# Attention logits of a two-layer graph network: FP32 products of 64 rows replaced by FP32R products of two-part queries and stacked two-part keys, with a smaller ring for software DMA

## The chip, the cores and the metric

The kernel runs on one core of one Trainium2 chip. The metric is the device time of one execution in microseconds; lower is better. A core has five engines with queues of their own: PE (TensorE, matrix products; PEld are its weight loads), DVE (VectorE), ACT (ScalarE), POOL (GpSimd) and SP (SyncE, which here only issues DMAs). Each works through its instructions in the order in which they were written, and waits where an operand is not there yet.

## The reference

Two layers over 4096 nodes with 256 features. Layer 0 is a graph attention with 4 heads over a dense adjacency `adj`, a residual and a layer norm. Layer 1 does two steps of a bilinear attention that keeps, in each row, the largest probabilities up to a mass of 0.9, and beside it a plain mixing with the adjacency. What matters here is the attention of layer 1:

```python
def _top_p_attention(X, W1, W2, W3):
    q = X @ W1.T @ W2.T            # (4096, 64)
    k = X @ W3.T                   # (4096, 64)
    logits = q @ k.T / TAU         # (4096, 4096), contraction over 64
    probs = jax.nn.softmax(logits, axis=-1)
    ...                            # keep the largest up to TOP_P = 0.9
    return A / jnp.maximum(A.sum(-1, keepdims=True), 1e-12)
...
for n in range(STEPS):             # STEPS = 2
    A = _top_p_attention(Xa, W1, W2, W3)
    Xf = R @ Xf                    # R: rows of S + identity, normalised
    Xa = A @ Xa
    Z = Z + Xf @ U1[n].T + Xa @ U2[n].T
```

Then come a residual and two layer norms.

## The kernel before

`graph_attention` does layer 0. For each of 8 heads (two halves of the columns, four heads) it goes over 32 pieces of 128 rows; a piece is a masked choice on DVE (L604, L607, 2.6 us each), two activations on ACT (L582, L589) and products into `acc` (L634). The inputs of the projections come in eight blocks `xt`; four of these lie for a time in the tile `kT` (`load_xT`, L217 to L224), which is not needed for keys yet. When a block of 512 nodes is done, it is normalised, and `Keys` (L427 to L466) transposes it, multiplies it with `w3` and puts the keys into `kT`. `w3` holds the same 64 columns twice, so the product `kp` has the keys in rows 0 to 63 and again in rows 64 to 127 of PSUM. ACT copies one of the halves (`evict`, L463): `kT` has 128 rows and 2048 columns, with the keys of nodes 0 to 2047 in the upper 64 rows and those of nodes 2048 to 4095 in the lower 64.

`nucleus_layer` does layer 1 in two steps of 32 row tiles (`RowTile`). Its helper `keys` (L859 to L881) makes the keys of the second step in the same layout, with a DVE copy at the end. A row tile runs through this:

- the query: transpose, product with `w1` (`front_q1`), product with `w2`, twice the same 64 columns (`front_q`, L908 to L914), so that the 128 rows of `q` are the 64 numbers of a query twice. ACT copies it from the PSUM bank `misc`, which in step 2 also serves the final products `zp` (L1352).
- the logits, in four "pairs" (`logits`, L917 to L932): one FP32 product for the block `pair` with the upper 64 rows and one for the block `pair + 4` with the lower 64 rows. The two use different rows of the array. Each has its PSUM bank; there are two banks of this kind (`ps_lg`, tag `lg`). `logits_evict` (L934) is two copies on ACT from these banks to the row tile `p`.
- the largest values of each chunk of 128 (`tops`, L939), the maximum (`top`), the exponentials (`spread`, `exp`), an estimate of the threshold in a few rounds (`estimate`, on DVE; in step 2 `estimate_half`, two passes over 2048 columns on ACT, L1040 and L1043), the exact threshold (`final`, `sort`, `edge`), the choice (`select` in step 1; `inside` and `cut` in step 2).
- the product with the features: transposes `tpa` (L1216), copies `at`, and 32 FP32 products `ap` (L1234).

Beside it `Mix` multiplies the adjacency with the features, `rp` (L1294): for most tiles as an F32R product with a low part of 258 columns (`low`) and an F16 product with a high part of 256 columns; `place_out` adds the last products `zp` (L1355), and layer norms.

The order of all this on PE, ACT, DVE and POOL is written out by hand: `at(time, part)` puts a part on a plan, in units of one row tile; `carry_out` sorts the plan by time and emits it. The due times are in the tables `T1` (step 1) and `T2` (step 2) at L1405 to L1411. The times say only the order within each engine. DMAs are on SP, apart from 32 mask loads (L556) and 8 casts from memory to memory (L211) on POOL, which convert as they move and so go through software DMA; all 40 are in layer 0.

At the end a flag counts rows for which the choice could not be confirmed; if it is not zero, a branch (L162) computes everything again in a general way (`graph_attention` without the factors, `nucleus_general`).

Of the kernel before, what the change touches and what calls it, by code (L numbers as in the profile page):

```python
# [22 lines left out]
P = 128  # L23
# [3 lines left out]
DA = 64  # L27
# [57 lines left out]
@with_exitstack  # L85
def tile_graph_layers(
    ctx: ExitStack,
    tc: tile.TileContext,
    x: bass.AP,
    xT: bass.AP,  # L90
    adjT: bass.AP,
    W: bass.AP,
    a: bass.AP,
    bias: bass.AP,
    res_w: bass.AP,
    res_b: bass.AP,
    W1T: bass.AP,
    W2T: bass.AP,
    W3T: bass.AP,
    U1T: bass.AP,  # L100
    U2T: bass.AP,
    ln_g: bass.AP,
    ln_b: bass.AP,
    out: bass.AP,
):
# [44 lines left out]
    graph_attention(  # L150
        tc, x, xT, adjT, W, a, bias, res_w, res_b, ident, eps, w3, kT, xf, x1_d, src_d, mask_d, adj_d,
        narrow, load_weights,
    )
    flag = const.tile([P, 1], I32, name="flag")
    nucleus_layer(
        tc, adjT, adj_d, adj32_d, high_d, low_d, w1, w2, w3, kT, U1T, U2T, ln_g, ln_b, ident, eps,
        xf, room, x1_d, xf1_d, xa2_d, narrow, flag, out,
    )


    missed = nc.values_load(flag[0:1, 0:1], min_val=0, max_val=STEPS * N)
    with tc.If(missed != 0):  # L162
        xf = room("xf_again")[:, :, : D + 1]
        graph_attention(
            tc, x, xT, adjT, W, a, bias, res_w, res_b, ident, eps, w3, kT, xf, x1_d, src_d, mask_d, adj_d,
            None, None,
        )
        nucleus_general(
            tc, adjT, w1, w2, w3, kT, U1T, U2T, ln_g, ln_b, ident, eps, xf, x1_d, xf1_d, out
        )  # L170


# [5 lines left out]

@with_exitstack
def graph_attention(  # L180
    ctx, tc, x, xT, adjT, W, a, bias, res_w, res_b, ident, eps, w3, kT, xf, x1_d, src_d, mask_d, adj_d,
    narrow, load_more,
):


# [31 lines left out]
    def load_xT(b):  # L217
        if b % 4 > 1:

            t = kT[:, b % 2 * 1024 : (b % 2 + 1) * 1024].rearrange("p (c n) -> p c n", c=2)  # L220
# [181 lines left out]
    def normalise(t0):  # L402
# [21 lines left out]

        return rest

    class Keys:  # L427


# [238 lines left out]
    for head in heads:  # L668
# [26 lines left out]
        for b in range(HB):  # L695
            at(time + 4.9 + b, head.add, b)
            if head.h == H - 1:

                k = b if head.half else 4 * b
                at(time + 5.2 + k, head.normalise, b)  # L700
                at(time + 6.7 + k, head.normalise_rest, b)
                parts = Keys(head.half * HB + b)
# [32 lines left out]
def nucleus_layer(  # L735
# [123 lines left out]
    def keys(b):  # L859

        xt = []
        for c in range(2):
            tp = ps_tr.tile([P, 512], F32, tag="tr", name=f"tpk{b}_{c}")
            for q in range(4):
                nc.tensor.transpose(
                    tp[:, q * P : (q + 1) * P], xa[:, b * 4 + q, c * P : (c + 1) * P], ident
                )
            t = two.tile([P, 512], F32, tag="at", name=f"xkt{b}_{c}", bufs=3)
            if c:
                nc.scalar.copy(t, tp)  # L870
# [8 lines left out]
        half, at = divmod(b, NB // 2)  # L879
        rows = slice(half * DA, (half + 1) * DA)  # L880
        nc.vector.tensor_copy(kT[rows, at * 512 : (at + 1) * 512], kp[rows, :])  # L881

    class RowTile:

# [23 lines left out]
        def front_q(self):  # L908
            qp = ps_one.tile([P, 512], F32, tag="misc", name=f"qq{self.id}")
            nc.tensor.matmul(  # L910
                qp[:, :P], w2.rearrange("p k a -> p (k a)"), self.q1, start=True, stop=True
            )
            self.q = two.tile([P, P], F32, tag="q", name=f"q_{self.id}")
            nc.scalar.copy(self.q, qp[:, :P])  # L914


        def logits(self, pair):  # L917

            if pair == 0:
# [6 lines left out]
            at = slice(pair * 512, (pair + 1) * 512)  # L926
            self.lps[pair] = []
            for half in range(2):
                lp = ps_lg.tile([P, 512], F32, tag="lg", name=f"lp{self.id}_{pair}_{half}")
                rows = slice(half * DA, (half + 1) * DA)  # L930
                nc.tensor.matmul(lp, self.q[rows, :], kT[rows, at], start=True, stop=True)  # L931
                self.lps[pair].append(lp)  # L932

        def logits_evict(self, pair):  # L934
            for half, lp in enumerate(self.lps.pop(pair)):
                b = half * (NB // 2) + pair
                nc.scalar.copy(self.p[:, b * 512 : (b + 1) * 512], lp)  # L937

        def tops(self, src, b):  # L939
# [265 lines left out]


        def tops_of_pair(self, pair):
            for half in range(2):
                self.tops(self.p, half * (NB // 2) + pair)

        def product_transpose(self, b):
            if b == 0:
# [188 lines left out]
    def at(time, part, *args):  # L1401
# [7 lines left out]
        lag=0.218, out=0.344, qt=0.253, q1=0.460, q2=0.612, space=0.125, apart=0.250, split=0.300,  # L1409
    )  # L1410
    T2 = dict(top=0.481, spread0=0.650, spread1=0.518, exp0=0.653, exp1=0.593, scalars=0.728, scalars2=0.769, est0=0.800, join0=0.820, move0=0.835, join1=0.945, move1=1.068, est2=1.200, join2=1.232, move2=1.395, lift=1.497, final=1.643, tops=1.647, sort=1.827, edge=2.032, inside=2.121, cut=2.230, product=2.354, lag=0.090, out=0.060, qt=-0.077, q1=0.461, q2=0.489, space=0.067, apart=0.074, mix=0.576, copy=0.042)  # L1411

    def carry_out():
        for _, _, part, args in sorted(plan, key=lambda e: e[:2]):
# [553 lines left out]
```

## Time and profile before

| | |
|---|---|
| median of 3 runs | 3505.24 us (3499.11 to 3508.46) |
| the profiled execution | 3507.4 us |
| its span, first to last instruction | 3505.5 us |
| mean granted clock of PE | 0.954 |
| busy time of PE, PEld, DVE, ACT, POOL | 3219.6, 2073.3, 2862.1, 2526.9, 610.9 us |
| products `rp` L1294, low and high part | 558.5 and 497.3 us |
| products `ap` L1234, step 1 and step 2 | 495.5 and 490.8 us |
| logits `lp` L931, 1024 records | 343.7 us |
| copies of the logits L937, 512 | 273.7 us |

A line of a group reads: line, engine, operation, output<-inputs, partitions x elements and type, count | busy time and mean ns of one | idle time of the engine just before them and what ended it. An FP32 product leaves two records on PE, an F32R or F16 product one. The ends of products are modelled from their starts, so that the mean of one is more than the distance from one to the next; where it matters, starts are compared. The slices cut the span into 40 parts of 87.6 us; a digit is the busy share in tenths.

### The profile page before, as it was taken

What the parts mean: (1) busy time and instruction counts of PE and PEld (TensorE: products, weight loads), DVE (VectorE), ACT (ScalarE), POOL (GpSimd) and SP (SyncE); (2) the same over time, 40 slices, a digit from 0 to 9 for tenths busy, and PEclk for the clock granted to TensorE, in tenths of its full rate; (3) what the DMA queues carried; (4) which work ended last, traced back from release to release, by engine and by line L of the source; (5) the groups of instructions that cost most, each with busy time, mean ns of one, the idle gap of its engine ahead of it and who ended that gap; (6) DMA issues with size and microseconds to landing.
All of it is one profiled execution on the core that took longest, in us unless ns stands there. A gap on an engine that the chain in (4) does not pass through costs nothing. (4 is left out here: it accounts for less than half of the span.)

```text
span 3505.5 us, 55976 instructions
## 1 busy us (share of the span) xinstructions
PE 3219.6 (92%) x19538; PEld 2073.3 (59%) x19538; DVE 2862.1 (82%) x8615; ACT 2526.9 (72%) x3970; POOL 610.9 (17%) x435
## 2 busy tenths in 40 slices
PE   8998888888789999999997899999899999999997
PEld 4522222222357777777774666666677777767775
DVE  4779989999658888888624998989989999988993
ACT  4678889888668888888715777777777677667752
POOL 1101450000000000000000222222223332332332
PEclk9999999999889999999998999999899999999988
DMA  9846443332242222222236444444644444444443
GB/s 213 136 113 140 128 133 119 110 112 85 74 132 103 106 82 103 106 94 92 100 99 165 120 113 118 121 117 120 166 104 109 109 118 107 112 108 108 111 106 82
DMA packets 637300, 402.58 MB, mean 115 GB/s; under 512 B 262672, under 2 KB 588304, under 8 KB 633936
## 3 DMA queue, kind: packets, MB, share of 16 engines
q1 hardware_dynamic: 626640, 315.03, 31.8%
q10 hardware_dynamic: 1536, 67.11, 5.3%
q0 software_dynamic: 8832, 16.78, 5.2%
q8 instruction: 155, 2.54, 0.3%
q14 instruction: 137, 1.12, 0.1%
HBM read 406.03 MB, written 118.62 MB: 150 GB/s over the span
## 5 line engine op out<-in xcount | busy, mean ns | idle before, releaser
L1294 PE MATMUL rp<-low,adj 128*128 128x258 f32 x1856 | 558.5, 390 | 29.3 <-ACT fx L1313 18.1
L1294 PE MATMUL rp<-p,short 128*128 128x256 f16 x1856 | 497.3, 295 | 1.5 <-DMA short<-adj_d 1.4
L1234 PE MATMUL ap<-xf,at 128*128 128x257 f32 x2048 | 495.5, 386 | 0.0
L604 DVE COPY_PREDICATED other<-mask,e 128x2048 f32<-128x2048 uint8 x176 | 451.3, 2574 | 52.7 <-ACT other L589 47.7
L1234 PE MATMUL ap<-xa,at 128*128 128x257 f32 x2048 | 490.8, 382 | 2.3 <-ACT at L1225 2.3
L1294 PEld LDWEIGHTS rp<-low,adj 128*128 128x128 f32 x1856 | 387.9, 209 | 141.9 <-issue 87.6
L1234 PEld LDWEIGHTS ap<-xf,at 128*128 128x128 f32 x2048 | 372.0, 190 | 133.8 <-ACT t L1110 22.7
L931 PE MATMUL lp<-kT,q 64*128 64x512 f32 x1024 | 343.7, 713 | 87.0 <-ACT p L937 86.6
L1225 ACT COPY at<-tpa 128x512 f32<-128x512 f32 x448 | 261.6, 584 | 220.3 <-PE tpa L1216 217.5
L582 ACT ACTIVATE e<-src,minus_flat,factors 128x2048 f32<-128x2048 f32 x176 | 368.1, 2091 | 65.4 <-DVE other L604 31.7
L634 PE MATMUL acc<-other,v 128*32 128x512 f32 x2816 | 343.2, 605 | 75.5 <-DVE other L604 64.5
L1234 PEld LDWEIGHTS ap<-xa,at 128*128 128x128 f32 x2048 | 373.0, 191 | 50.3 <-ACT at L1225 3.7
L589 ACT ACTIVATE other<-away,minus_flat 128x2048 f32<-128x2048 f32 x176 | 350.8, 1993 | 7.2 <-PE acc L634 6.2
L1204 POOL TENSOR_TENSOR p<-p,w 128x1024 f32<-128x1024 f32 x128 | 300.0, 2364 | 255.6 <-DVE w L1200 233.0
L937 ACT COPY p<-lp 128x512 f32<-128x512 f32 x512 | 273.7, 585 | 90.4 <-PE lp L931 89.6
L1216 PE MATMUL tpa<-ident,p 128*128 128x128 f32 x2048 | 312.5, 276 | 1.4 <-POOL p L1204 1.4
L1216 PEld LDWEIGHTS tpa<-ident,p 128*128 128x128 f32 x2048 | 248.0, 142 | 41.9 <-issue 6.4
L1200 DVE MATCH_REPLACE8 w<-c,w 128x128 f32<-128x128 f32 x1024 | 268.0, 276 | 0.0
L955 ACT ACTIVATE junk_s<-p,htop 128x2048 uint8<-128x2048 f32 x128 | 256.1, 2000 | 10.1 <-DVE htop L950 10.1
L634 PEld LDWEIGHTS acc<-other,v 128*32 128x32 f32 x2816 | 80.7, 110 | 303.2 <-DVE other L604 151.1
L966 ACT ACTIVATE p<-p,ntop 128x2048 f32<-128x2048 f32 x128 | 257.4, 2011 | 1.0
L941 DVE MAX8 c<-p 128x8 f32<-128x128 f32 x1024 | 209.6, 277 | 58.8 <-ACT p L937 55.6
(268 smaller groups left out, 5359.0 us busy)
## 6 DMA issues: line engine op xcount, KB each, us to landing
adj<-adj_d SPq DMA_DIRECT2D x464, 256.0 KB
mask<-adj_d SPq DMA_DIRECT2D x164, 256.0 KB
short<-adj_d SPq DMA_DIRECT2D x232, 128.0 KB
mask<-mask_d SPq DMA_DIRECT2D x60, 256.0 KB
adj<-in_adjT SPq DMA_DIRECT2D x48, 256.0 KB
mask<-in_adjT POOLq DMA_DIRECT2D x32, 256.0 KB, 7.8
adj_d<-mask SPq DMA_DIRECT2D x32, 256.0 KB
src<-src_d SPq DMA_DIRECT2D x8, 1024.0 KB
```

Of the source, the lines that this page charges most:

```text
L582: nc.scalar.activation(self.e, self.head.src, AF.Relu, scale=self.factor(0), bias=self.factor(2))
L589: nc.scalar.activation(self.other, self.head.away, AF.Identity, bias=self.factor(2))
L604: nc.vector.copy_predicated(self.other, self.mask, self.e)
L634: nc.tensor.matmul(head.acc[k][at : at + 32, :], weights, self.e[:, b * 512 : (b + 1) * 512], tile_position=(0, at), **ends,)
L931: nc.tensor.matmul(lp, self.q[rows, :], kT[rows, at], start=True, stop=True)
L937: nc.scalar.copy(self.p[:, b * 512 : (b + 1) * 512], lp)
L1200: nc.vector.match_replace(w[:, cols], self.cand[:, c * TOP : (c + 1) * TOP], w[:, cols], 0.0)
L1204: nc.gpsimd.tensor_tensor(self.p[:, cols], self.p[:, cols], w[:, cols], ALU.subtract)
L1216: nc.tensor.transpose(tp[:, q * P : (q + 1) * P], self.p[:, (b * 4 + q) * P : (b * 4 + q + 1) * P], ident,)
L1225: nc.scalar.copy(at, tp)
L1234: nc.tensor.matmul(self.ap[:, : D + 1], at[:, q * P : (q + 1) * P], self.cur[:, j, :], start=j == 0, stop=j == NT - 1,)
L1294: nc.tensor.matmul(self.rp[:, : part.shape[1]], a, part, start=start and k == 0, stop=stop and k == len(parts) - 1,)
```

## The change

The keys and queries are split in two FP32R parts each, a rounded one and what is left. `kT` becomes an FP32R tile of 128 rows and 4096 columns: the upper 64 rows are the first part of the keys, the lower 64 the second part. `q` becomes a tile of two FP32R queries, first part and second part, each with its 64 numbers twice over the 128 rows. A block of logits is now two FP32R products of all 128 rows into one bank, with the first and the second part of the query as weights; together they have all four products of parts. So a "pair" is four products of 512 columns where it was two FP32 ones, and it covers the neighbouring blocks `2 * pair` and `2 * pair + 1`.

For the split, ACT copies all 128 rows of the key product and a DVE subtraction puts the rest into the lower 64 rows (`evict_rest`, and the end of `keys`); ACT copies the query and a DVE subtraction makes its second part (`front_q_rest`, due at `q3`). The four blocks `xt` that lay in `kT` now lie in a tile `landing` of FP32 that takes turns with `kT` in one place. The tables T1 and T2 get an entry `q3`, and T2's due times shift a little. `kT` and `q` take more room in each partition; the ring for software DMA is set to 4096 bytes.

```diff
-    kT = const.tile([P, N // 2], F32, name="kT")
+    def keys(name, dtype=F32R):
+        return const.tile([P, N], dtype, tag="kT", name=name)
+
+    landing, kT = keys("landing", F32), []
...
         def evict(self):
-            half, at = divmod(self.b, NB // 2)
-            rows = slice(half * DA, (half + 1) * DA)
-            nc.scalar.copy(kT[rows, at * 512 : (at + 1) * 512], self.kp[rows, :])
+            if not kept:
+                kept.append(keys())
+            self.part = kept[0][:, self.b * 512 : (self.b + 1) * 512]
+            nc.scalar.copy(self.part, self.kp)
+
+        def evict_rest(self):
+            rest = self.part[DA:]
+            nc.vector.tensor_tensor(rest, self.kp[DA:, :], rest, ALU.subtract)
...
                 at(time + 11.8 + k, parts.evict)
+                at(time + 12.3 + k, parts.evict_rest)
...
-        nc.vector.tensor_copy(kT[rows, at * 512 : (at + 1) * 512], kp[rows, :])
+        part = kT[:, b * 512 : (b + 1) * 512]
+        nc.scalar.copy(part, kp)
+        nc.vector.tensor_tensor(part[DA:], kp[DA:, :], part[DA:], ALU.subtract)
...
-            self.q = two.tile([P, P], F32, tag="q", name=f"q_{self.id}")
-            nc.scalar.copy(self.q, qp[:, :P])
+            self.q = two.tile([P, 2, P], F32R, tag="q", name=f"q_{self.id}")
+            self.qp = qp[:, :P]
+            nc.scalar.copy(self.q[:, 0], self.qp)
+
+        def front_q_rest(self):
+            nc.vector.tensor_tensor(self.q[:, 1], self.qp, self.q[:, 0], ALU.subtract)
...
-            for half in range(2):
-                lp = ps_lg.tile([P, 512], F32, tag="lg", name=f"lp{self.id}_{pair}_{half}")
-                rows = slice(half * DA, (half + 1) * DA)
-                nc.tensor.matmul(lp, self.q[rows, :], kT[rows, at], start=True, stop=True)
-                self.lps[pair].append(lp)
+            for b in (2 * pair, 2 * pair + 1):
+                lp = ps_lg.tile([P, 512], F32, tag="lg", name=f"lp{self.id}_{b}")
+                for k in range(2):
+                    nc.tensor.matmul(
+                        lp,
+                        self.q[:, k],
+                        kT[:, b * 512 : (b + 1) * 512],
+                        start=k == 0,
+                        stop=k == 1,
+                    )
+                self.lps[pair].append((b, lp))
...
T1:  + q3=0.680
T2:  top 0.481 -> 0.468, spread1 0.518 -> 0.516, exp0 0.653 -> 0.655, exp1 0.593 -> 0.607,
     scalars 0.728 -> 0.731, est0 0.800 -> 0.808, join0 0.820 -> 0.810, move0 0.835 -> 0.828,
     move1 1.068 -> 1.088, est2 1.200 -> 1.144, lift 1.497 -> 1.491, final 1.643 -> 1.649,
     tops 1.647 -> 1.651, sort 1.827 -> 1.842, edge 2.032 -> 2.034, inside 2.121 -> 2.135,
     qt -0.077 -> -0.086, q1 0.461 -> 0.421, q2 0.489 -> 0.453, + q3=0.523
...
+        at(time + T["q3"], t.front_q_rest)
...
-    nc = bacc.Bacc("TRN2", target_bir_lowering=False, num_devices=1)
+    nc = bacc.Bacc(
+        "TRN2", target_bir_lowering=False, num_devices=1, dynamic_dma_scratch_size=4096
+    )
```

In the branch that computes everything again, layer 0 lands its blocks in the same way and makes no keys, and the general layer uses the landing tile for its own keys, as before in FP32.

More of the change, by code (lines that the diff above doesn't have):

```diff
@@ L150, in tile_graph_layers @@
     graph_attention(
-        tc, x, xT, adjT, W, a, bias, res_w, res_b, ident, eps, w3, kT, xf, x1_d, src_d, mask_d, adj_d,
-        narrow, load_weights,
+        tc, x, xT, adjT, W, a, bias, res_w, res_b, ident, eps, w3, landing,
+        lambda: kT.append(keys("kT")) or kT[0], xf, x1_d, src_d, mask_d, adj_d, narrow, load_weights,
     )
@@ L155, in tile_graph_layers @@
     nucleus_layer(
-        tc, adjT, adj_d, adj32_d, high_d, low_d, w1, w2, w3, kT, U1T, U2T, ln_g, ln_b, ident, eps,
+        tc, adjT, adj_d, adj32_d, high_d, low_d, w1, w2, w3, kT[0], U1T, U2T, ln_g, ln_b, ident, eps,
         xf, room, x1_d, xf1_d, xa2_d, narrow, flag, out,
@@ L163, in tile_graph_layers @@
         xf = room("xf_again")[:, :, : D + 1]
+        landing = keys("landing_again", F32)
         graph_attention(
-            tc, x, xT, adjT, W, a, bias, res_w, res_b, ident, eps, w3, kT, xf, x1_d, src_d, mask_d, adj_d,
-            None, None,
+            tc, x, xT, adjT, W, a, bias, res_w, res_b, ident, eps, w3, landing, None, xf, x1_d, src_d,
+            mask_d, adj_d, None, None,
         )
         nucleus_general(
-            tc, adjT, w1, w2, w3, kT, U1T, U2T, ln_g, ln_b, ident, eps, xf, x1_d, xf1_d, out
+            tc, adjT, w1, w2, w3, landing, U1T, U2T, ln_g, ln_b, ident, eps, xf, x1_d, xf1_d, out
         )
@@ L180, in graph_attention @@
 def graph_attention(
-    ctx, tc, x, xT, adjT, W, a, bias, res_w, res_b, ident, eps, w3, kT, xf, x1_d, src_d, mask_d, adj_d,
-    narrow, load_more,
+    ctx, tc, x, xT, adjT, W, a, bias, res_w, res_b, ident, eps, w3, landing, keys, xf, x1_d, src_d,
+    mask_d, adj_d, narrow, load_more,
 ):
@@ L218, in load_xT @@
         if b % 4 > 1:
-            t = kT[:, b % 2 * 1024 : (b % 2 + 1) * 1024].rearrange("p (c n) -> p c n", c=2)
+            t = landing[:, b % 2 * 1024 : (b % 2 + 1) * 1024].rearrange("p (c n) -> p c n", c=2)
         else:
@@ L425, in normalise @@
         return rest
+    kept = []
     class Keys:
@@ L701, in graph_attention @@
                 at(time + 6.7 + k, head.normalise_rest, b)
+                if keys is None:
+                    continue
                 parts = Keys(head.half * HB + b)
@@ L878, in keys @@
             )
-        half, at = divmod(b, NB // 2)
-        rows = slice(half * DA, (half + 1) * DA)
-        nc.vector.tensor_copy(kT[rows, at * 512 : (at + 1) * 512], kp[rows, :])
+        part = kT[:, b * 512 : (b + 1) * 512]
+        nc.scalar.copy(part, kp)
+        nc.vector.tensor_tensor(part[DA:], kp[DA:, :], part[DA:], ALU.subtract)
     class RowTile:
@@ L925, in logits @@
                 self.cand = two.tile([P, NC * TOP], F32, tag="cand", name=f"c{self.id}", bufs=3)
-            at = slice(pair * 512, (pair + 1) * 512)
             self.lps[pair] = []
-            for half in range(2):
-                lp = ps_lg.tile([P, 512], F32, tag="lg", name=f"lp{self.id}_{pair}_{half}")
-                rows = slice(half * DA, (half + 1) * DA)
-                nc.tensor.matmul(lp, self.q[rows, :], kT[rows, at], start=True, stop=True)
-                self.lps[pair].append(lp)
+            for b in (2 * pair, 2 * pair + 1):
[9 more added lines that the diff above has]
+                self.lps[pair].append((b, lp))
         def logits_evict(self, pair):
-            for half, lp in enumerate(self.lps.pop(pair)):
-                b = half * (NB // 2) + pair
+            for b, lp in self.lps.pop(pair):
                 nc.scalar.copy(self.p[:, b * 512 : (b + 1) * 512], lp)
@@ L1207, in tops_of_pair @@
         def tops_of_pair(self, pair):
-            for half in range(2):
-                self.tops(self.p, half * (NB // 2) + pair)
+            for b in (2 * pair, 2 * pair + 1):
+                self.tops(self.p, b)
         def product_transpose(self, b):
@@ L1408, in nucleus_layer @@
         move1=1.853, lift=1.861, final=1.897, sort=1.983, edge=2.281, select=2.299, product=2.548,
-        lag=0.218, out=0.344, qt=0.253, q1=0.460, q2=0.612, space=0.125, apart=0.250, split=0.300,
+        lag=0.218, out=0.344, qt=0.253, q1=0.460, q2=0.612, q3=0.680, space=0.125, apart=0.250, split=0.300,
     )
-    T2 = dict(top=0.481, spread0=0.650, spread1=0.518, exp0=0.653, exp1=0.593, scalars=0.728, scalars2=0.769, est0=0.800, join0=0.820, move0=0.835, join1=0.945, move1=1.068, est2=1.200, join2=1.232, move2=1.395, lift=1.497, final=1.643, tops=1.647, sort=1.827, edge=2.032, inside=2.121, cut=2.230, product=2.354, lag=0.090, out=0.060, qt=-0.077, q1=0.461, q2=0.489, space=0.067, apart=0.074, mix=0.576, copy=0.042)
+    T2 = dict(top=0.468, spread0=0.650, spread1=0.516, exp0=0.655, exp1=0.607, scalars=0.731, scalars2=0.769, est0=0.808, join0=0.810, move0=0.828, join1=0.945, move1=1.088, est2=1.144, join2=1.232, move2=1.395, lift=1.491, final=1.649, tops=1.651, sort=1.842, edge=2.034, inside=2.135, cut=2.230, product=2.354, lag=0.090, out=0.060, qt=-0.086, q1=0.421, q2=0.453, q3=0.523, space=0.067, apart=0.074, mix=0.576, copy=0.042)
     def carry_out():
```

## The prediction

> **What bounds the kernel now.** I read the page first: shares, the 40 slices, the groups; then the table by stage, the chain of waits, and the timeline around the logits. Three stages stand out in the slices: graph attention (0 to 950 us), the first nucleus step (950 to 1815) and the second (1860 to 3345, with a tail after it).
>
> ```profile
> PE   8998888888789999999997899999899999999997
> DVE  4779989999658888888624998989989999988993
> PEclk9999999999889999999998999999899999999988
> ...
> L931 PE MATMUL lp<-kT,q 64*128 64x512 f32 x1024 | 343.7, 713 | 87.0 <-ACT p L937 86.6
> ```
>
> ```profile
> 950.00:1815.00 865.00, 847.50 (x4171) 629.70 (x4168) 630.40 (x2310) 641.91 (x1264) 35.30 (x68) 0.98 0.30 104
> 1860.00:3345.00 1485.00, 1362.30 (x7688) 1024.77 (x7686) 1317.36 (x5254) 1061.75 (x2046) 408.85 (x251) 0.94 0.47 119
> ```
>
> The second fence is the table by stage; its columns are window, length, busy time of PE, PEld, DVE, ACT, POOL, granted clock, DMA share, GB/s. In step 1 PE is busy 847 of 865 us (and 200 of every 200 from 1100 to 1700); DVE and ACT stand at 73%. That stage is PE's. In step 2 PE has 92%, DVE 89%, and the clock is down to 0.94: neither bounds it alone. The chain of waits (it goes back to 2528 us) names PE for 18% of the span, DVE 4%, ACT 4%; `lp` L931 has 1.9%, 67 us.
>
> The logits themselves, from PE's timeline in step 1, with an accumulating product `ap` ahead and behind:
>
> ```profile
> 1299.98 1.90 PE L1234 MATMUL ap<-xf,at 128*128 128x257 f32 x8
> 1301.72 0.60 PE L1216 MATMUL tpa<-ident,p 128*128 128x128 f32 x4
> ...
> 1302.46 1.13 PE L931 MATMUL lp<-kT,q 64*128 64x512 f32 x4
> 1303.52 2.00 PE L1234 MATMUL ap<-xf,at 128*128 128x257 f32 x8
> ```
>
> Ends are modelled, so I count from start to start. A pair of blocks (four records: an FP32 matmul has two, and two matmuls of 64 rows each stand side by side in the array) takes 1303.52 - 1302.46 = 1.06 us. Eight `ap` records take 1.74, so 0.2175 us for 257 columns. The key products have the width of the logits but use all 128 rows; their weight loads follow each other by one record:
>
> ```profile
> 942.48 0.19 PEld L455 LDWEIGHTS kp<-xk,w 128*128 128x128 f32 x1 [0.24 <-issue]
> 942.91 0.19 PEld L455 LDWEIGHTS kp<-xk,w 128*128 128x128 f32 x1 [0.24 <-issue]
> 943.34 0.19 PEld L455 LDWEIGHTS kp<-xk,w 128*128 128x128 f32 x1 [0.24 <-issue]
> ```
>
> That is 0.43 us a record of 512 columns, each with a load of its own that costs nothing. Two records side by side, twice, would be 0.86; the logits take 1.06. So 0.20 us a pair is lost, 0.10 at each change of weights in the half arrays.
>
> Last, step 2 around the third pair of a tile:
>
> ```profile
> 2565.61 1.13 PE L931 MATMUL lp<-kT,q 64*128 64x512 f32 x4
> 2567.99 2.00 ACT L1043 ACTIVATE junk_s<-p,t 128x2048 uint8<-128x2048 f32 x1
> 2570.17 1.05 ACT L937 COPY p<-lp 128x512 f32<-128x512 f32 x2
> 2570.79 2.56 PE L931 MATMUL lp<-kT,q 64*128 64x512 f32 x4 [2.87 <-ACT p L937]
> ```
>
> ```profile
> 2572.00:2578.00 6.00, 6.00 (x18) 2.53 (x15) 6.00 (x47) 2.24 (x6) 5.66 (x3) 0.50 0.15 45
> ```
>
> ACT is busy with two passes of 2 us (L1040, L1043) between the copies; PE has both logits banks full and waits 2.87 us. Then the granted clock is 0.50, and the pair takes 2.5 us instead of 1.06. Nearly every tile of step 2 shows this; PE's waits for this copy sum to 70.4 us between 1950 and 3300.
>
> **The change part by part.** The profiled execution took 3507.4 us, its span 3505.5, so 1.9 lie around it; the median of the runs is 3505.24, 2.2 less. I sum against 3507.4 and take off 2.
>
> *FP32R matmuls.* A pair is still four records, now of 128 rows and 512 columns, one after the other. The price of such a column: `low` (F32R, 258 columns) and the high part (F16, 256) alternate in L1294. From 2566.67 to 2567.43 three of them take 0.76, 0.25 us a couple; at half clock (2573.75 to 2574.65, two couples) 0.45. The difference, 0.20, is what the clock governs: 514 columns at 0.4 ns, half of the 0.84 of an FP32 record. The other 0.05 a couple is fixed. So a record of 512 columns is 0.215, and four are 0.86 with hidden loads (as `ap` and `kp`), 0.96 with half of the fixed 0.05 on each. The upper end is 1.26, if each of the four loses 0.10 as the 64-row ones do; the lower end is 0.86. I take 0.89, nearest to the FP32 rows with 128-row loads: 0.17 less a pair.
>
> "FP8 and Floating Point Precision", section "TensorE Precision Notes" of the Trainium skill has a true FP32 product make four passes through the array. By that rule alone two half arrays with four passes and four matmuls of one pass take the same time and the gain would be 0; the measured 1.06 against 0.86 is a loss that the rule does not count.
>
> *Step 1:* 32 tiles x 4 pairs x 0.17 = 22 us, all on PE's path, since PE waits for nobody there (wait 0.4 us before all its logits). Next late is DVE at 82% in the steady stretch; it keeps slack.
>
> *Step 2:* the pairs take 199 us there from start to start (192.9 busy), against 128 x 1.06 = 136 undisturbed. An undisturbed one gains 0.17, 22 us in all. A pair at half clock gains more: 4 x 0.43 = 1.72 instead of 2.0 to 2.5, and its first bank is done after two records, so that ACT's copy starts about 0.4 us (at full clock) earlier. About half the pairs are disturbed; with 0.4 for these it is 64 x 0.17 + 64 x 0.4 = 36. Of the `lp` time after 2528 (some 88 us) the chain carries 67, 76%: 27 us.
>
> *DVE, `front_q_rest` (64 times):* 128 columns from PSUM. Between L1156 (48 wide, 0.208) and L1381 (256 wide, 0.425) lies 0.29 us. Step 1 hides 32 x 0.29 = 9 us in DVE's idle 27%; uncovered it would cost 9. There it is queued behind ACT's copy L914, and the estimates behind it start up to 0.9 us later: in the stretch from 1300 on the selection ends at 1306.93 and PE's next transpose after the logits at 1308.65 is at 1313.29, 6 us later, so PE does not see it. In step 2 DVE is near its limit: 0 to 9, I take 7. The bank `misc` stays taken until this subtraction. In the out phase the next user is `zp`: DVE is free for it at 2995.46, `zp` starts at 3000.12, so 4 us are to spare. POOL and SP get nothing new.
>
> *Keys:* 8 subtractions of 0.69 (as L881, 512 columns from PSUM) in each step. In stage 0 DVE is at 95% (500 to 840 us): four there cost 2.8, the four at the end hide behind the query chain (946.7 to 949.6). ACT's copy of 128 rows costs what 64 cost (L937 585 ns, L466 578). Before step 2, ACT's copy plus the subtraction stand where one DVE copy stood; a mixing product of 1.7 us after each block covers it, except the last: +1. First query +0.3. Sum +4, from 0 to +10.
>
> *Ring for software DMA:* 32 mask loads (7.8 us each to landing, one every 4.3 us on the average) and 8 casts (15.6, one every 46). A few at once, loaded seven pieces ahead. Cost 0. Were they forced one after the other: 32 x (7.8 - 4.3) = 112 us, partly hidden; nothing in the rows hints at it.
>
> *Landing tile:* another buffer for the same four loads, free long before the keys: 0. Due times T2: small shifts that make room for the third query part; the two ACT passes stay between the first and second copy, so the wait stays. 0, with 15 to each side.
>
> Sum: 3507.4 - 22 - 27 + 7 + 4 = 3469.4; less 2 for the median: 3468.
>
> **Rivals.** (1) *More gain in step 2.* Its clock is 0.94 over 1485 us, so 89 us worth of clock are lost, half of it reachable if PE's waits fall under the point at which the clock drops. For: the first bank is released earlier. Against: ACT's two passes start no earlier. About 45 more: 3425. (2) *No difference.* DVE takes over step 2 (it is idle only some 127 us of 1350 from 1950 to 3300), PE's gain there is lost: 3507 - 22 + 7 + 4 - 2 = 3494; or the pair keeps its 1.06 through loads of two-part weights: 3507 + 11 - 2 = 3516. (3) *Slower by the clock.* Place: the third pair of each step-2 tile. PE reaches it 0.35 us sooner, the ACT copy does not; waits of 2.1 to 2.7 us (most tiles after 2770, which show one 3.4 us stretch at 0.5) become waits around 3, and those (1987 to 2528) mostly show 6.8 us at 0.5. It decides when the wait passes some 2.9 us. Price: 16 tiles x 1.7 us clock + 32 x 0.35 waiting = 38, and the gain in step 2 is gone: 3505 - 22 + 11 + 38 = 3532. Against: the shorter pairs behind it. (4) *Loads not hidden.* Four x 0.10: the pair takes 1.26, +0.20, 128 pairs in each step: +26, +20, +11: 3562.
>
> Rival 4 has a page behind it: "TensorE: Matmul & The Clock Gate", section "Part 3: Packing small matmuls — row/col tiling" of the Trainium skill lets a weight load overlap running matmuls only where the row groups differ, which would make four full-array loads show. The trace speaks the other way round: `kp`, same row group, hides its loads (0.43 a record), and the 64-row logits, different row groups, lose 0.10 each.
>
> (5) *It does not do what it says:* the parts are not exact enough, the flag at the end is set and the general branch runs; that computes both layers again, thousands of us.
>
> **Chances.** 0.3% is 10.5 us, about what a measurement of this kernel can tell from no change. Forecast (3468, 3440 to 3492) 0.51; rival 1 0.14; rival 2 0.14, nearly all within 0.3%; rival 3 0.13; rival 4 0.06; rival 5 0.02. So faster 0.65, same 0.14, slower 0.21. The range goes from 3415 (rival 1 with its margin) to 3535 (rival 3).
>
> **What would show it.** Four `lp` records from start to start: 0.89 (0.86 to 0.96) in step 1; 1.06 or 1.26 would fell the sum. Tiles of step 1 every 23.05 us instead of 23.75, PE still without waits. In step 2: DVE's busy time up by 9 us, PE's wait before the third pair within 0.4 of today's, granted clock 0.94 or more. If it falls under 0.92, rival 3 is at work. A wait of `zp` for DVE, or of POOL between its loads, would be costs that I set to 0.

## The result, and the profile after

The changed kernel takes **3445.31 us** (median of 4 runs, 3444.52 to 3446.17), the kernel before took 3504.56 beside it (4 runs, 3499.11 to 3508.46): a ratio of 0.9832 with a 95% interval of 0.9815 to 0.9849. That is 59 us or 1.7% faster; 37 us were forecast. The span fell from 3505.5 to 3444.2 us.

The same lines of the page as before, now of the kernel after (slices, shares of the chain of waits, the group of the logits):

```profile
PE   8998888888889999999997898989899999999986
DVE  4779989999848888888714999999999999899983
PEclk9999999999989999999998999999999999999998
...
PE 14%; DVE 14%; ACT 3%; issue 2%; POOL 0%; DMA 0%; DVEq 0%; POOLq 0%; ACTq 0%
...
L950 PE MATMUL lp<-kT,q 128*128 128x512 f32 x1024 | 339.7, 458 | 106.0 <-ACT p L961 105.6
```

In slices 22 to 28 (counted from 0, all in step 2) PE now reads 8 and 9 in turn, where it read 9 from 23 to 27, and DVE reads 9 from slice 22 to 33, where it fell to 8 three times. On the chain DVE now has as large a share as PE, 14% each (18% and 4% before). In the last line look at the end, not at the busy time: the busy time of `lp` has hardly fallen (343.7 to 339.7), because half-array records that ran side by side before were counted once, and because the ends are modelled. The idle time ahead of the logits grew from 87 to 106 us.

Where the 61 us went is read from the first and last record of `lp` in each step:

| stretch | before, us | after, us | change |
|---|---|---|---|
| start to the first `lp` | 949.6 | 955.1 | +5.5 |
| step 1, first to last `lp` | 768.8 | 728.9 | -39.9 |
| last `lp` of step 1 to the first of step 2 | 139.1 | 138.4 | -0.8 |
| step 2, first to last `lp` | 1485.2 | 1458.1 | -27.1 |
| from there to the end | 162.8 | 163.7 | +0.9 |

The table by stage for the two steps of the kernel after (window, length, busy time of PE, PEld, DVE, ACT, POOL with counts, granted clock, DMA share, GB/s):

```profile
955.00:1684.00 729.00, 714.44 (x3683) 601.00 (x3684) 607.71 (x2258) 608.54 (x1206) 31.19 (x63) 0.98 0.31 108
...
1822.00:3280.00 1458.00, 1305.78 (x7689) 1064.13 (x7689) 1321.04 (x5260) 1062.66 (x2047) 409.46 (x251) 0.94 0.48 122
```

Step 1 is still PE's: 714 of 729 us, DVE at 83%. In step 2 DVE now has 91% and PE 90%. Over the same stretch of step 2 (first to last `lp`) PE's busy time fell from 1362.3 to 1305.8, by 56.5 us, but its idle time grew by 29.5, and DVE's idle time shrank from 169.6 to 137.0. So half of the busy time that PE saved in step 2 became waiting.

### The profile page after: what moved, and what is told of

Its sections match the earlier page's. It is cut to its first block, busy times and chain, and to the rows that moved or that the text cites. A ratio compares the mean times of both kernels' runs of the same rounds, so it can differ in the third digit from the quotient of the medians.

```text
span 3444.2 us, 56052 instructions
## 1 busy us (share of the span) xinstructions
PE 3120.7 (91%) x19538; PEld 2162.0 (63%) x19538; DVE 2881.3 (84%) x8687; ACT 2528.7 (73%) x3978; POOL 611.2 (18%) x435
## 5 line engine op out<-in xcount | busy, mean ns | idle before, releaser
L1318 PE MATMUL rp<-low,adj 128*128 128x258 f32 x1856 | 542.8, 382 | 26.7 <-ACT fx L1337 14.6
L1258 PE MATMUL ap<-xf,at 128*128 128x257 f32 x2048 | 483.5, 380 | 0.0
L950 PE MATMUL lp<-kT,q 128*128 128x512 f32 x1024 | 339.7, 458 | 106.0 <-ACT p L961 105.6
L1318 PEld LDWEIGHTS rp<-low,adj 128*128 128x128 f32 x1856 | 387.9, 209 | 49.3 <-ACT fx L1337 20.7
L1258 PEld LDWEIGHTS ap<-xf,at 128*128 128x128 f32 x2048 | 381.1, 190 | 55.1 <-DVE at L1247 0.3
L950 PEld LDWEIGHTS lp<-kT,q 128*128 128x128 f32 x1024 | 193.6, 212 | 152.0 <-ACT p L961 119.2
```

Of the source, the lines that this page charges most:

```text
L950: nc.tensor.matmul(lp, self.q[:, k], kT[:, b * 512 : (b + 1) * 512], start=k == 0, stop=k == 1,)
L1258: nc.tensor.matmul(self.ap[:, : D + 1], at[:, q * P : (q + 1) * P], self.cur[:, j, :], start=j == 0, stop=j == NT - 1,)
L1318: nc.tensor.matmul(self.rp[:, : part.shape[1]], a, part, start=start and k == 0, stop=stop and k == len(parts) - 1,)
```

## Where step 1 gained more than the pair

PE's timeline in step 1, kernel after (start, length, engine, line, operation, count):

```profile
1301.93 1.90 PE L1258 MATMUL ap<-xf,at 128*128 128x257 f32 x8
1303.67 0.60 PE L1240 MATMUL tpa<-ident,p 128*128 128x128 f32 x4
1304.03 1.19 PE L950 MATMUL lp<-kT,q 128*128 128x512 f32 x4
1305.05 1.90 PE L1258 MATMUL ap<-xf,at 128*128 128x257 f32 x8
1306.79 0.60 PE L1240 MATMUL tpa<-ident,p 128*128 128x128 f32 x4
```

and before, around a pair with the same neighbours:

```profile
1319.90 0.60 PE L1216 MATMUL tpa<-ident,p 128*128 128x128 f32 x4
1320.43 1.13 PE L931 MATMUL lp<-kT,q 64*128 64x512 f32 x4
1321.49 2.00 PE L1234 MATMUL ap<-xf,at 128*128 128x257 f32 x8
1323.33 0.60 PE L1216 MATMUL tpa<-ident,p 128*128 128x128 f32 x4
```

From start to start the pair takes 1305.05 - 1304.03 = 1.02 us, not 0.89: 0.04 less than the 1.06 of before. Yet a tile of step 1 comes every 22.70 us instead of 23.79, 1.09 less, or 0.27 a pair. The rest is in the neighbours. The eight `ap` behind the pair take 1306.79 - 1305.05 = 1.74 us from start to start; before, eight `ap` behind a pair took 1.84 (1321.49 to 1323.33), and 1.74 elsewhere. On average over the steady tiles (from the fourth on they are alike), the first record behind the logits went from 0.321 to 0.216 us, and the last records ahead of the four pairs of a tile (`tpa` twice, `tp_x`, `qp`) sum to 0.29 us instead of 0.81, 0.13 less a pair: the four `tpa` above take 0.36 (1303.67 to 1304.03), where four of them take 0.43 elsewhere and took 0.53 ahead of a pair before. So 0.04 + 0.105 + 0.13 makes about 0.27: most of the gain stands outside the records of the logits.

Inside the four FP32R records the distances are 324, 235, 235 and 229 ns. The first, behind records of another type, is 0.09 us longer than the others, but it also starts sooner behind its neighbour; the first experiment below measures by how much.

## The experiments

Three theories were open after the result. **Edges:** the gain of step 1 comes from leaving half arrays. The rival is that FP32R itself, with one record instead of two for a product, gives it. **DVE bounds step 2:** a shorter pair brings nothing more there. The rivals are the new subtraction, the retuned due times, or PE's wait before the third pair. **Keys:** the stretch before the first `lp` grew by the subtractions. Single runs of one kernel differ by 5 to 13 us, so differences under some 5 us are left open.

### Type and rows of the logits, one thing at a time

**FP32 with all 128 rows.** The second half of the query's rows is made zero (`w2`), so that each block is one FP32 product of 128 rows; there is no subtraction for the keys, and nothing is left out of the logits. The layout of the blocks and the due times are those of the kernel after.

```diff
-                for k in range(2):
-                    nc.tensor.matmul(lp, self.q[:, k], kT[:, ...], start=k == 0, stop=k == 1)
+                nc.tensor.matmul(lp, self.q[:, 0], kT[:, ...], start=True, stop=True)
...
-    def keys(name, dtype=F32R):
+    def keys(name, dtype=F32):
...
-            nc.sync.dma_start(w2[:, k, :], W2T)
+            if k == 0:
+                nc.sync.dma_start(w2[:, k, :], W2T)
+            else:
+                nc.gpsimd.memset(w2[:, k, :], 0.0)
```

> FP32 logits over all 128 rows: the keys twice in the rows, the lower half of the query zero (exact, half of the work idle), four records of 512 columns a block pair, in the layout and due times of the changed kernel, without the subtraction of the keys. Theory: the half arrays cost 0.10 to 0.13 us at the entry and 0.10 at the exit of each pair, by loads that show in the neighbours' records; with all rows they are hidden: a pair takes 4 x 0.43 = 1.72, the record after the logits is at its usual 0.22 (0.86 a tile) and the last one before at 0.06 to 0.11; tile of step 1 22.70 + 4 x 0.70 = 25.5. Rival: the edges belong to FP32 products of this width: then they stay (1.28 and 0.8 a tile) and the tile takes 26.4.

Measured: 3544.89 us (one run), a tile of step 1 every 25.83 us, where 25.5 was expected if the edges go and 26.4 if they stay.

```profile
1310.53 1.90 PE L1255 MATMUL ap<-xf,at 128*128 128x257 f32 x8
1312.27 0.60 PE L1237 MATMUL tpa<-ident,p 128*128 128x128 f32 x4
1312.71 1.88 PE L951 MATMUL lp<-kT,q 128*128 128x512 f32 x4
1314.43 1.90 PE L1255 MATMUL ap<-xf,at 128*128 128x257 f32 x8
1316.16 0.60 PE L1237 MATMUL tpa<-ident,p 128*128 128x128 f32 x4
```

The pair now takes 1.745 us on average over the steady tiles (1.72 here), four records of 0.43 one after the other. The eight `ap` behind it take 1316.16 - 1314.43 = 1.73 and the four `tpa` ahead of it 0.44: as elsewhere, though the type is still FP32. Over a tile the records ahead sum to 0.53, between the 0.81 of half arrays and the 0.29 of FP32R. So both edges belong to the half arrays, 0.07 a pair ahead and 0.105 behind. The other 0.06 ahead is FP32R's: its first record starts sooner. That, and a third pair that is longer (1.82 us behind `qp`), make up the difference from 25.5 to 25.83.

The run says something on step 2 as well. Its pairs are longer than those of before, yet step 2 took 1471.6 us from first to last `lp`, 13.6 less than before, with 68 us at half clock where the kernel before had 182. Four traces of one and the same step 2 (the kernel after twice, the later keys' subtraction below twice) lie between 1450.2 and 1458.2. So a shorter pair is not the only thing that shortens step 2; the rows, the layout of the blocks and the due times changed here too, and this one run does not tell them apart.

**Half arrays with FP32R.** Only the first parts of query and keys, in two products of 64 rows side by side; the second parts, and the subtractions for the keys, are left out.

```diff
-            for b in (2 * pair, 2 * pair + 1):
+            for half in range(2):
+                b = 2 * pair + half
...
+                rows = slice(half * DA, (half + 1) * DA)
+                nc.tensor.matmul(lp, self.q[rows, 0], kT[rows, ...], start=True, stop=True)
```

> F32R logits in half arrays: one product of 64 rows a block, two side by side, first parts alone (the rests of keys and queries are left out of the logits). Theory: the edges belong to the half arrays: they come back (first record after the logits 1.28 us a tile instead of 0.86, last before them 0.8 instead of 0.3); a pair takes 0.23 to 0.33 plus edges, the tile 20.5 us. Rival: they belong to FP32: no edges, the tile 19.6 to 19.8, where DVE and ACT set it.

Measured: 3412.67 us (one run), a tile every 21.92 us, where 20.5 was expected.

```profile
1307.67 0.60 PE L1236 MATMUL tpa<-ident,p 128*128 128x128 f32 x4
1308.20 0.50 PE L950 MATMUL lp<-kT,q 64*128 64x512 f32 x2
1308.63 2.00 PE L1254 MATMUL ap<-xf,at 128*128 128x257 f32 x8
1310.47 0.60 PE L1236 MATMUL tpa<-ident,p 128*128 128x128 f32 x4
```

With half arrays both edges are back: four `tpa` take 0.53, eight `ap` 1.84, and over a tile the last records ahead sum to the 0.81 of the kernel before. The two products start 3 ns apart and take 0.43 us till the next record starts, nearly as long as two FP32R products of all rows one after the other (0.229 to 0.235 each). Why the tile is longer than expected is told by the next run.

**One product a block.** All 128 rows, the second query part left out of the products.

```diff
-                for k in range(2):
-                    nc.tensor.matmul(lp, self.q[:, k], kT[:, ...], start=k == 0, stop=k == 1)
+                nc.tensor.matmul(lp, self.q[:, 0], kT[:, ...], start=True, stop=True)
```

> The changed kernel with the first query part alone: one product of 512 columns for each block, so two records a pair; the logits lack the second part, the subtraction on DVE stays. Theory: a pair takes half of 1.02, 0.51 us, and step 1 stays PE's: tiles of 20.7 us instead of 22.7, 62 us less in step 1. In step 2 DVE (94% busy) does not follow: 5 to 20 us less there. Rival: step 2 is still set by PE: 50 us or more less there too.

Measured: 3418.15 us (3415.7 and 3420.7), ratio 0.9759 (0.9734 to 0.9784). A tile of step 1 takes 21.91 us, not 20.7: the records of `lp` fell from 4.09 to 2.42 us a tile, but PE now waits. Step 1 is 22 us shorter than in the kernel after, where 62 were expected.

```profile
1304.13 2.00 PE L1253 MATMUL ap<-xf,at 128*128 128x257 f32 x8
1306.55 2.00 PE L1253 MATMUL ap<-xf,at 128*128 128x257 f32 x8 [0.42 <-DVE at L1242]
```

Such waits of `ap` for the copies `at` come 28 times, 12.1 us, in a step 1 where there were none. The half-array kernel stops at the same 21.9, with 28 such waits, 11.0 us. That is the next limit of step 1: 0.8 us a tile below the kernel after. In step 2, half of the logits' products are gone and the stretch takes 1450.2 us, 8 less than after. With less work for PE than in the kernel after, step 2 hardly gets shorter.

### What bounds step 2

**No subtraction on DVE for the query.** The second product takes a tile of zeros as its weights; the second query part is left out, PE has the same work.

```diff
-            nc.vector.tensor_tensor(self.q[:, 1], self.qp, self.q[:, 0], ALU.subtract)
...
-                        self.q[:, k],
+                        zero_r if k else self.q[:, 0],
```

> The changed kernel without the subtraction of the query on DVE; a constant tile of zeros stands for the second part, so the logits lack that part (PE does the same work). Theory: DVE covers it in step 1 (0 us there), in step 2 it costs at most its own 32 x 0.29 = 9 us: total 0 to 9 us faster, 3436 to 3445. If step 2 is now bound by DVE alone, it is the 9; if PE still sets it, near 0. Rival: the waits of DVE for ACT's copy of the query (33.6 us in 34 waits) are paid too: 30 us faster or more.

Measured: 3440.72 us (3433.6 to 3443.9), ratio 0.9824 (0.9801 to 0.9846); tile of step 1 22.68, step 2 1449.4 us. Step 1 hides the subtraction, as forecast. Step 2 is 8.7 us shorter than in the kernel after; the subtraction's own time there is 32 x 0.29 = 9.3. But the next run, which keeps the subtraction, is as short, so this is not separated from the spread. The rival, 30 us or more, falls.

**Due times of before.** T2 as before the change, with `q3=0.559`.

> The changed kernel with the due times T2 of the kernel before, and the new query part at 0.559 (0.07 after the second). Theory: the gain in step 2 (1485 us from its first to its last logits before, 1458 after) comes from the shorter pairs, and the new due times only make room: the time stays at 3445 within 10 us. Rival: the moved due times brought the gain of step 2: then some 25 us slower, 3470, all of it in step 2, with step 1 at 22.7 us a tile in both cases.

Measured: 3438.59 us (3428.2 to 3439.5), ratio 0.9809 (0.9786 to 0.9833). The retuned times of step 2 bring nothing; step 2 takes 1450.0 us with the old ones, against 1458.1. Whether the old ones are a few us better stays open.

**Three banks for the logits**, two instead of three for the transposes.

```diff
-        tc.tile_pool(name="f_lg", bufs=2, ...
+        tc.tile_pool(name="f_lg", bufs=3, ...
-        tc.tile_pool(name="f_tr", bufs=3, ...
+        tc.tile_pool(name="f_tr", bufs=2, ...
```

> The changed kernel with three PSUM banks for logits and two for transposes. Theory: in step 2 PE waits for ACT's copies before the third pair (105.6 us over the kernel) and then runs at half clock; with a bank more, half of that pair can run ahead: waits and half clock fall, but DVE is 94% busy in step 2: 5 to 15 us faster, 3430 to 3440. Rival: two banks for transposes cost more than that, in step 1 above all, where PE is the bound: 10 us or more slower.

Measured: 3444.44 us (3442.8 to 3449.6), ratio 0.9839 (0.9819 to 0.9859): no gain, where 5 to 15 us were expected. PE's waits before the logits fell only from 105.6 to 93.4 us: one bank more removes little of the wait behind ACT's two passes.

**The copy first.** The second of ACT's two passes (`estimate_half`) is due 0.03 behind `move`, so that it stands behind the copy of the second pair.

```diff
-                at(time + T2[f"move{k - 1}"] + 0.002, t.estimate_half)
+                at(time + T2[f"move{k - 1}"] + (0.002 if k == 1 else 0.03), t.estimate_half)
```

> The changed kernel with the second estimate's two ACT passes due after the copy of the second logits pair instead of before it (0.03 instead of 0.002 behind the move). Theory: step 2 is DVE's now, PE's waits before the third pair (105.6 us over the kernel) cost little: they shrink by half or more, the granted clock of step 2 rises from 0.94 to 0.96 or more, and the time stays within 10 us. Rival: these waits and the half clock behind them still set step 2: 20 us or more faster. Third: the estimate comes later, DVE waits for it: slower by some 32 x 1.2 = 38 us.

Measured: 3445.46 us (3442.8 to 3448.7), ratio 0.9828 (0.9812 to 0.9845); the kernel after on the same chip, below, 3444.91. PE's waits in step 2 of the kernel after (waiting <- what it waits for: us in all, times, longest):

```profile
PE lp L950 <- ACT p L961: 103.8, 34, 5.8
PE rp L1318 <- ACT fx L1337: 14.6, 17, 2.7
PE qp L918 <- DVE h L1405: 10.7, 10, 2.7
```

and in step 2 with the copy first, and its line of the table by stage:

```profile
PE lp L950 <- ACT p L961: 53.5, 21, 4.6
PE zp L1379 <- ACT t_o L835: 27.2, 13, 3.0
PE qp L918 <- DVE h L1405: 24.8, 12, 3.5
```

```profile
1822.00:3280.00 1458.00, 1296.51 (x7701) 1054.75 (x7699) 1321.68 (x5267) 1059.40 (x2053) 410.68 (x251) 0.96 0.48 122
```

This was the test of rival 3's wait. It was halved, the time at half clock in step 2 fell from 160 us (the kernel after, measured beside it) to 114, the granted clock rose from 0.94 to 0.96, and the time of the kernel is the same; step 2 itself took 1453.7 us against 1458.2, within the spread of its traces. PE waits elsewhere instead: `zp` for ACT 27.2, which is not among the waits of the kernel after in step 2, and `qp` for DVE 24.8. DVE's busy time is the same to 0.7 us. So neither PE's wait for the copy nor the half clock that follows it sets the end of step 2 in the kernel after; what is left, with the largest busy share (91%), is DVE. That DVE's order of work bounds it is supported by this and by the one product, but not shown: no run here took a large piece off DVE in step 2 alone. A chain of waits that runs through DVE and ACT in turn is not excluded either.

### Keys and ring

**The ring alone:** the kernel before with the smaller ring.

```diff
-    nc = bacc.Bacc("TRN2", target_bir_lowering=False, num_devices=1)
+    nc = bacc.Bacc(
+        "TRN2", target_bir_lowering=False, num_devices=1, dynamic_dma_scratch_size=4096
+    )
```

> The kernel before with the ring for software DMA at 4096 bytes and nothing else changed. Theory: 0, 3505 within 5 us, and the software DMAs land after 7.8 and 15.6 us as before. Rival: a smaller ring holds back POOL's loads: slower by up to tens of us in the first 500 us, or it is the reason why the second head starts 3 us earlier in the changed kernel: then 3 us faster.

Measured: 3499.87 us (10 runs, 3490.5 to 3510.1), ratio 0.9991 (0.9975 to 1.0007). No effect on the time; the mask loads land after 8.1 us instead of 7.8, as in the kernel after.

**The keys' subtraction later** (first half of layer 0 only).

```diff
-                at(time + 12.3 + k, parts.evict_rest)
+                at(time + (12.3 if head.half else 14.3) + k, parts.evict_rest)
```

> The changed kernel with the key subtraction of the first half of stage 0 due two pieces later (14.3 instead of 12.3). Theory: stage 0 grew by 5.5 us, 8 of it between the starts of heads 4 and 5 (112.7 us before, 120.8 after), because DVE, which bounds this stage, waits for ACT's copy there (6.8 us in 4 waits) besides the 2.8 us of the four subtractions: some 6 us faster, 3439. Rival: the 8 us come from something else in that head (masks, the wider copy): no difference.

Measured: 3435.94 us (3429.0 to 3441.0), ratio 0.9817 (0.9797 to 0.9836). The reason is in DVE's timeline and waits of the kernel after, between 507 and 630 us:

```profile
551.39 0.69 DVE L479 TENSOR_TENSOR kT<-kp,kT 64x512 fp32r<-64x512 f32 x1 [2.05 <-ACT kT L475]
```

```profile
DVE kT L479 <- ACT kT L475: 6.8, 4, 3.6
```

The subtraction is ready in the order of DVE before ACT has made its copy, and the masked choices queue behind it: DVE stands for 6.8 us in 4 waits. With the later due time these four waits are gone.

**Again, side by side with the kernel after** (5 runs each, one chip), and a kernel with both moves: the later subtraction and the due times of before.

> The changed kernel once more, beside the three others of this call. Single runs of the earlier variants lie up to 13 us apart and stage 0 and step 2 each differ by 8 to 15 us between traces of the same code there, so the small differences need the same chip: 3445 within 5 us if the first result is typical, 3438 if it was at the upper end.

> The key subtraction of the first half of stage 0 two pieces later, again. Theory: DVE's waits there (6.8 us) go, 6 to 7 us faster than the changed kernel of this call. Rival: the earlier 9 us were the spread of the runs: within 2 us of it.

> The later key subtraction together with the due times T2 of the kernel before (new query part at 0.559). Theory: the later subtraction gives its 6 us, the old due times 0 to 7: 6 to 13 us faster than the changed kernel of this call. Rival: neither is more than the spread: within 3 us of it.

| kernel | us, median (lowest to highest) | ratio (95%) | first `lp` at |
|---|---|---|---|
| the kernel after | 3444.91 (3437.6 to 3448.7) | 0.9820 (0.9803 to 0.9837) | 956.3 |
| keys' subtraction later | 3437.45 (3433.5 to 3445.4) | 0.9808 (0.9789 to 0.9828) | 948.1 |
| that and the old due times | 3437.21 (3427.7 to 3438.0) | 0.9794 (0.9776 to 0.9812) | 952.2 |

By medians the later subtraction is 7.5 us faster, about as much as DVE waited (6.8); the intervals overlap. Seven traces with the due time of the change have the first `lp` between 953 and 958 us, three with the later one between 940 and 952. That speaks for it more than the medians do. The two kernels without any subtraction of the keys have it at 943 and 945. The old due times add nothing that can be told from the spread (3437.21 against 3437.45).

## Why the prediction came near, point by point

- **Direction and bound: right.** Step 1 was PE's and gained, PE still nearly without waits (idle 14 us of 729, 17 of 769 before); step 2 gained less than PE saved. The range, 3415 to 3535, holds the result.
- **Pair of step 1, 0.89 us: too low.** Its own records take 1.02, near the 1.06 by which I said the sum would fall. Less the 0.06 by which its first record starts sooner, it costs the path 0.96, which is the upper value that the fixed part of `low` and `high` gave (0.86 and 4 x 0.025). The row that I took as nearest, FP32 with hidden loads, was the wrong one of the two.
- **Step 1, -22 us: too small, for a reason I had not in the sum.** It came to -39.9. The tiles give 32 x 1.09 = 35; a pair gained 0.10 by its price (1.06 to 0.96), where 0.17 was forecast, and about 0.175 by the edges of half arrays, ahead and behind, where the sum had nothing. I had looked for the loss of half arrays inside the pair alone (0.10 at each change of weights). The edges were in the trace of before, 1.84 against 1.74 for the same eight `ap`, and I had read one of the two. So a pair priced too cheap and edges left out partly cancelled: that the total lies inside the forecast's narrower range, 3440 to 3492, is in part luck. Forecast tile 23.05, measured 22.70. The other 5 us of step 1 lie in its first three tiles, which differ by a few us from trace to trace; their cause is open.
- **Step 2, -27 on PE and +7 on DVE: net 20 forecast, 27 measured.** The size is near, but this is in part luck too, since the way there is not as told. PE's busy time fell by 56.5 us and 29.5 came back as idle time. The subtraction takes 290 ns, as forecast; DVE's busy time rose by 5.7 us in a step 27 us shorter. DVE's waits for PE's `zp` fell from 27.8 to 15.3 us and those for ACT's `halves` from 40.1 to 14.7, while others grew. FP32 with all rows took 13.6 us off step 2 with a longer pair, and one product instead of two took only 8 us more off it than the change did. Which part of the 27 belongs to which term stays open.
- **Rival 1, more gain by the clock:** not what happened. The granted clock of step 2 stayed at 0.94 and PE's waits grew. The copy first raised the clock to 0.96 and the kernel gained no time.
- **Rival 2, DVE takes over step 2:** half right. The runs support that it happened, but only after 27 us were gained; the 3494 of this rival had none.
- **Rival 3, slower by the clock:** its wait grew (PE before the logits from 86.6 to 105.6 us) and its price did not come: time at half clock in step 2 went from 182 to 170 us and the granted clock stayed at 0.94. The edge that it put at a wait of some 2.9 us is not sharp in the trace of before: waits of 2.28, 2.35 and 2.39 us stand at stretches of 6.8 us at 0.5 as well, and one of 3.08 at a stretch of 3.4. The copy first shows why the waits cost nothing now: PE has the slack.
- **Rival 4, loads not hidden: wrong, as forecast.** Four loads of all rows, two for each block, are hidden in records of 0.23 us. "TensorE: Matmul & The Clock Gate", section "Part 3: Packing small matmuls — row/col tiling" of the Trainium skill lets loads overlap only where row groups differ. These traces show the reverse, full rows with hidden loads (0.229 to 0.235 us a record), and half arrays with a loss of about 0.10 us at each change.
- **The general branch** was not taken: the kernel takes 3445 us, and the branch was put at thousands of us more. Rival 5 falls.
- **Four passes for FP32**, which "FP8 and Floating Point Precision", section "TensorE Precision Notes" of the Trainium skill states, agrees with the FP32 products of all rows: 1.745 / 2 = 0.87 us a block, 3.7 to 3.8 times the 0.229 to 0.235 of an FP32R product. By that rule alone the change would have gained nothing. In step 1 the gain is what half arrays lost inside the pair (0.20) and at its edges (0.175), less the 0.10 that the four FP32R records, with their sooner start, take over 0.86.
- **Keys, +4: 2.4 too little before the first `lp`.** +5.5 came there, where 2.8 + 0.3 were forecast. The subtractions cost what I said (0.695 us), but the wait for ACT's copy ahead of them, 6.8 us, was left out: I had set the price of the instruction and not asked what stands behind it when its operand is late. Before step 2 the subtraction waits 21.9 us in 8 times without harm (-0.8 in that stretch). The subtractions and the wait make 9.6 us, more than the 5.5: the two kernels without this subtraction reach the first `lp` 5 to 6 us sooner than the kernel before, and why is not shown.
- **`misc` bank, cost 0: not quite.** `zp` waits no longer than before (12.6 us, 12.1 before), but `q1`, moved from 0.461 to 0.421, now waits for DVE (`qp` for `h`, 10.7 us in 10 waits). With the old time the kernel is no slower and perhaps a few us faster.
- **Ring, landing tile, due times, 0: right** for the ring (0.9991) and for T2 within its 15. The mask loads land after 8.1 us, 7.8 before. The landing tile was not tried alone.
- **Two slips in the adding up**, without weight: 3469.4 less 2 is 3467, and 45 less than 3468 is 3423.

## What to carry to other kernels

Price a record with its neighbours: compare the same group of instructions where it stands behind the disputed one and where it does not, since a change of shape or type is paid by the next record. When one engine gets faster in a stage where two are near their limit, ask at once how much of the other's idle time is left, because the rest of the gain turns into waits that look like a new problem and cost nothing. And a short instruction added on a busy engine costs its wait for its operand, in front of everything queued there; place it behind the point where the operand is ready.

## What the runs showed of the hardware beyond that

- Two FP32 products of 64 rows side by side cost the full-array record behind them 0.105 us (0.321 instead of 0.216) and the one ahead 0.07 on the average, 0.09 where it is a `tpa` or `tp_x` (0.203 instead of 0.109) and nothing where it is `qp`; with FP32 and all rows these records take 0.217 and 0.109.
- FP32R: the first of four 512-column products after another type takes 0.324 us to the next start and begins 0.06 sooner on the average than an FP32 one; the others take 0.235, 0.235 and 0.229, with a weight load each that does not show.
- Two FP32R products of 64 rows took 0.43 us for both, edges beside, with starts 3 ns apart. Whether they overlap and pay for the change of weights, or do not overlap, is not told apart by these runs.
- A stage can gain granted clock (0.94 to 0.96) without the kernel gaining time, where PE is no longer what bounds it.
